# An attention and mixture-of-experts block: queries and keys projected feature-major, tile fronts ranked ahead, modulation rows spread by DMA

## The chip, the cores and the metric

The kernel runs as one program on one core of a Trainium2 chip. The metric is device time in microseconds (us) of one execution. The engines are named as in the profile: PE is TensorE's matrix multiply and PEld its weight loads, DVE is VectorE, ACT is ScalarE, POOL is GpSimd, SP is SyncE, which mostly issues DMA transfers. An engine name with a q (ACTq, SPq) is that engine's instruction queue.

## The reference

A block over 2 sequences of 2048 tokens with 256 features: adaptive layer norm, causal attention with two query heads of 128 that share one key and one value head, and then a dense-weighted mixture of 8 experts. Cut to what matters:

```python
mod = (silu(c) @ wmod).reshape(2, 6, 1, 256)
sa, ca, ga, sb, cb, gb = six rows of mod          # per sequence
ga = (2 * (ga >= 0) - 1) * maximum(abs(ga), 0.25) # gb likewise
h = layernorm(x) * (1 + ca) + sa
q, k, v = rope(h @ Wq.T), rope(h @ Wk.T), h @ Wv.T  # rope turns neighbouring pairs of features
w = softmax(causal(q @ k.T * 128 ** -0.5))
x = x + ga * ((w @ v) @ Wo.T)
h = layernorm(x) * (1 + cb) + sb
gate = softmax(h @ Wg + bg) - sigmoid(h @ Wt + bt) * 0.125   # kept where >= 0, renormalised
x = x + gb * sum over experts of gate_e * (gelu(h @ W1_e + b1_e) @ W2_e + b2_e)
```

All inputs and outputs are 32-bit floats, and so are the matmuls of the projections, scores and experts.

## The kernel before, in words

The program has two stages. `attention` works through 32 tiles of 128 tokens (16 in each sequence); `experts` then runs over lists of the tokens that each expert was given.

**How the order comes about.** In `attention` nothing is issued when the Python code passes it. Each step is handed to a `Plan` with `plan.add(engine, cost, what to do, after=..., take=..., give=..., rank=...)`. `Plan.run` plays a list schedule with these costs: whenever an engine is free, it takes the ready step of lowest rank, provided that the buffers it takes are free by the counts in `room`. What comes out is a fixed order of instructions on each engine; on the chip each engine follows its order strictly and waits on semaphores. `late` is an allowance for a transfer's landing. `first` is the rank -100 for the steps of the start.

**A tile** (`tile_steps`) has rank `r`, and all its steps share that rank. It loads x on SP, takes mean and variance (`moments`: L432 and L434 on DVE, L438 and L439 on POOL), normalises (`xn`, L468 on DVE or POOL), turns the tile by two PE transposes (`turn`, L477), and applies scale and shift while it copies to hT (L485 on ACT, L487 on DVE). `qkv` (L498) multiplies hT, as the stationary side, with the joined weight matrix of 512 columns: two matmuls with 512 moving columns. An f32 matmul is executed as two passes, so that is four records in the trace. The result lies with tokens on the partitions. `rot` forms the rotation from it on DVE (L514, L520, L523), the two products are added on DVE or POOL (L529), and `turn_rot` (L536) turns the two queries and the key by three PE transposes so that features lie on the partitions; `qT_out` (L539, L541) copies them out on ACT, the queries scaled by 128 ** -0.5.

The rest of a tile is scores (`score`, L552, and the mask by a bf16 matmul, L556), maximum (L563 and L570 on DVE), exponential (L579 on ACT), transposes of the probabilities (L625) and copies (L629), the product with the values (`pav`, L635), a copy (L663), the output projection (`po`, L669), the residual sum (L676), the second norm (`hx`, L692 and L695), a store of the token's features in planes of 16 bits (`halves`, L702) and the gating logits (`pl`, L739). After every group of up to four tiles `gate_steps` works out which experts take each token, and POOL scatters entries into the list of expert 0 (L852).

**Modulation.** `by_feature` (L342) gives the first norm's scale and shift with features on the partitions. For each of the two sequences, `gates` (L365) and `rows` (L393) multiply c, copied over 128 columns (`sc_bc`, L333), with the other modulation weights, so that every partition receives the same rows; `gates_out` (L374 to L388) applies sign and minimum on all 128 partitions and folds the gate into the output weights woG.

**Buffers.** Six PSUM banks serve as "ps", two as "pav"; 16 score buffers "s", 9 input tiles "x".

**The end of attention.** Steps of rank 1000 work on two items of expert 0 ahead (`pha` L1007, `pya` L1024) while the last tiles' gating, lists and gathers run. Then `experts` starts.

Of the kernel before, what the change touches and what calls it, by code (L numbers as in the profile page):

```python
# [12 lines left out]
F32 = mybir.dt.float32  # L13
# [8 lines left out]
P = 128  # L22
# [17 lines left out]
MASKED = -3.0e38  # L40
HB = 6
# [162 lines left out]
def attention(  # L204
# [9 lines left out]
            "hT": 2, "hT2": 2, "hpT": 2, "aT": 2, "g_sb": 1, "sign": 1, "size": 1, "ga": 1}  # L214
    const = ctx.enter_context(tc.tile_pool(name="const_a", bufs=1))
    pool = ctx.enter_context(tc.tile_pool(name="work", bufs=3))
    small = ctx.enter_context(tc.tile_pool(name="small", bufs=8))
# [9 lines left out]
    def little(shape, tag, u, dtype=F32):  # L227
        return small.tile(shape, dtype, tag=tag, name=f"{tag}{u}")
# [19 lines left out]
    wqkv_sb = const.tile([P, KD, 4 * HS], F32, name="wqkv_sb")  # L248
# [5 lines left out]
    rope_sb = const.tile([P, NT, 2, HS // 2], F32, name="rope_sb")  # L254
# [5 lines left out]
    wo_sb = wpool.tile([P, NH, D], F32, tag="w2_0", name="wo_sb")  # L260
    sc_bc = wpool.tile([P, KD, B, P], F32, tag="w1_0", name="sc_bc")
# [12 lines left out]
    nc.vector.tensor_copy(back[:, 0, :], ids)  # L274
    nc.gpsimd.memset(kept.front, 0.0)
    nc.gpsimd.memset(entry, 0.0)
    nc.gpsimd.tensor_copy(
        entry[:, :, :, 2].bitcast(I32), ids.unsqueeze(2).to_broadcast([P, NTOK // P, E])
    )
    for z in (1, 0):  # L280
        nc.vector.tensor_scalar(back[:, z, :], back[:, 0, :], float(z - NTOK), None, ALU.add)
# [8 lines left out]
    def idle_work(many):  # L290
        pi = ps_tile(f"pi{many}")
        for _ in range(many):
            nc.tensor.matmul(pi[:, :P], ident, ident, start=True, stop=True)

    plan.add("PE", 5.0, lambda: idle_work(12), take=["ps"], give=["ps"], rank=first - 5)
# [4 lines left out]
    l_m0 = load(wm_0, wm[:, :, : 2 * D], 512, rank=first - 1)  # L300
    l_qkv = load(wqkv_sb, wqkvT.rearrange("(k p) f -> p k f", p=P), 512, rank=first - 1)
    l_rope = [
        load(rope_sb[:, ds(4 * q, 4)], rope.rearrange("(q n p) (z f) -> p q n z f", p=P, n=4, z=2)[:, q],
             256, rank=first if q == 0 else q * 8 - 7.5)
        for q in range(NT // 4)
    ]
# [13 lines left out]
    def load_expert(e):  # L320
# [10 lines left out]
    s_bc = plan.add(  # L331
        "DVE", 0.6,
        lambda: nc.vector.tensor_copy(sc_bc, sc.unsqueeze(3).to_broadcast([P, KD, B, P])),  # L333
        after=[s_sc], rank=first,
    )
# [22 lines left out]
    m_wo, m_mod, m_gb = [], [], []  # L358
    for b in range(B):

        def gates(b=b):
            box["pg", b] = pg = ps_tile(f"pg{b}")
            for g, which in enumerate((2, 5)):
                for k in range(KD):
                    nc.tensor.matmul(  # L365
                        pg[:, ts(g, D)], sc_bc[:, k, b, :], wm_1[:, k, ts(which - 2, D)],
                        start=(k == 0), stop=(k == KD - 1),
                    )

        def gates_out(b=b):  # L370

            u = f"_g{b}"
            g_sb = work([P, 2 * D], "g_sb", u)
            nc.vector.tensor_copy(g_sb, box["pg", b])  # L374
            sign = work([P, 2 * D], "sign", u)
            nc.vector.tensor_scalar(sign, g_sb, 0.0, 2.0, ALU.is_ge, ALU.mult)
            size = work([P, 2 * D], "size", u)
            nc.vector.scalar_tensor_tensor(size, g_sb, -1.0, g_sb, ALU.mult, ALU.max)
            nc.vector.tensor_scalar(size, size, 0.25, None, ALU.max)
            ga = work([P, D], "ga", u)  # L380
            nc.vector.scalar_tensor_tensor(
                ga, sign[:, :D], 1.0, size[:, :D], ALU.subtract, ALU.mult
            )
            nc.vector.scalar_tensor_tensor(
                gb_bc[:, b, :], sign[:, D:], 1.0, size[:, D:], ALU.subtract, ALU.mult
            )
            for h in range(NH):
                nc.vector.tensor_tensor(woG[:, b, h, :], wo_sb[:, h, :], ga, ALU.mult)  # L388

        def rows(b=b):  # L390
            box["pr", b] = pr = ps_tile(f"pm2{b}")
            for k in range(KD):
                nc.tensor.matmul(  # L393
                    pr, sc_bc[:, k, b, :], wm_1[:, k, D : 3 * D],
                    start=(k == 0), stop=(k == KD - 1),
                )

        def rows_out(b=b):
            pr = box["pr", b]
            nc.vector.tensor_copy(mod_bc[:, b, :D], pr[:, :D])  # L400
            nc.vector.tensor_scalar(mod_bc[:, b, D:], pr[:, D:], 1.0, None, ALU.add)

        r = 1.6 + 3 * b
        g = plan.add("PE", 1.8, gates, after=[s_bc, l_m1], take=["ps"], rank=r)
        m_wo.append(plan.add("DVE", 4.0, gates_out, after=[g, l_wo], give=["ps"], rank=r))
        g = plan.add("PE", 1.8, rows, after=[s_bc, l_m1], take=["ps"], rank=r)
        m_mod.append(plan.add("DVE", 0.9, rows_out, after=[g], give=["ps"], rank=r))

    prev, l_first = [], []
    for e in range(RES):  # L410
        prev = [
            plan.add(
                "SP", 6.0, lambda e=e: load_expert(e), after=m_wo + m_mod + [m_T] + prev, late=2.0,
                rank=8.0 + 4 * e,
            )
        ]
        l_first += prev
# [26 lines left out]
    def tile_steps(b, i, r, group, g):  # L444
# [9 lines left out]

        def load_x():
            st["x"] = work([P, D], "x", u)
            nc.sync.dma_start(st["x"], x[b, ts(i, P), :])
# [6 lines left out]
        n_n = moments("a" + u, st, [n_x], add)  # L464
# [7 lines left out]
        n_n = add(["DVE", "POOL"], [0.42, 1.3], xn, [n_n], take=["xn"])  # L472
# [16 lines left out]
        n_t = add("PE", 0.32, turn, [n_n], take=["ps"], give=["xn"])  # L489
        n_0 = add("ACT", 0.27, lambda: hT(0, "ACT"), [n_t, m_T], take=["hT"])  # L490
        n_1 = add(
# [3 lines left out]
        def qkv():  # L495
            st["pq"] = ps_tile(f"pq{u}")
            for k in range(KD):
                nc.tensor.matmul(  # L498
                    st["pq"], st["hT"][:, k, :], wqkv_sb[:, k, :],
                    start=(k == 0), stop=(k == KD - 1),  # L500
                )

        n_q = add("PE", 1.75, qkv, [n_0, n_1, l_qkv], take=["ps"], give=["hT"])
        n_v = add("ACT", 0.27, lambda: nc.scalar.copy(v[:, i, :], st["pq"][:, 3 * HS :]), [n_q])
        ready_v[b, i] = n_v


        def rot(z):
            dst = st["t", z] = work([P, 3, HS], f"t{z}", u)
            table = rope_sb[:, i, z, :]  # L510
            src = st["pq"][:, : 3 * HS].rearrange("p (h j two) -> p h j two", h=3, two=2)
            d4 = dst.rearrange("p h (j two) -> p h j two", two=2)
            if z == 0:
                nc.vector.tensor_tensor(  # L514
                    d4, src,
                    table.unsqueeze(1).unsqueeze(3).to_broadcast([P, 3, HS // 2, 2]), ALU.mult,
                )
            else:
                t3 = table.unsqueeze(1).to_broadcast([P, 3, HS // 2])
                nc.vector.scalar_tensor_tensor(  # L520
                    d4[:, :, :, 0], src[:, :, :, 1], -1.0, t3, ALU.mult, ALU.mult
                )
                nc.vector.tensor_tensor(d4[:, :, :, 1], src[:, :, :, 0], t3, ALU.mult)  # L523

        n_r0 = add("DVE", 0.6, lambda: rot(0), [n_q, l_rope[i // 4]], take=["big"])
        n_r1 = add("DVE", 0.75, lambda: rot(1), [n_q, n_v, n_r0], give=["ps"])
        n_r = add(
            ["DVE", "POOL"], [0.58, 1.0],
            lambda eng: of[eng].tensor_tensor(st["t", 0], st["t", 0], st["t", 1], ALU.add),  # L529
            [n_r0, n_r1],  # L530
        )

        def turn_rot():
            st["pr"] = ps_tile(f"pr{u}")
            for h in (2, 0, 1):
                nc.tensor.transpose(st["pr"][:, ts(h, P)], st["t", 0][:, h, :], ident)  # L536

        def qT_out():
            nc.scalar.copy(kT[:, ts(i, P)], st["pr"][:, 2 * P : 3 * P])  # L539
            st["qT"] = work([P, NH, P], "qT", u)  # L540
            nc.scalar.mul(st["qT"].rearrange("p h t -> p (h t)"), st["pr"][:, : NH * P], scale)  # L541

        n_t = add("PE", 0.48, turn_rot, [n_r], take=["ps"], give=["big"])
        n_k = add("ACT", 0.65, qT_out, [n_t], take=["qT"], give=["ps"])
# [13 lines left out]
        def keep(h, c):  # L558
            w = min(SC, n - c * SC)
            s = st["s", h, c] = work([P, SC], "s", f"{u}_{h}_{c}")  # L560
            if ("mx", h) not in st:
                st["mx", h] = little([P, 4], "mx", f"{u}_{h}")
            nc.vector.tensor_scalar(  # L563
                s[:, :w], st["sc", h, c][:, :w], 1.0, None, ALU.mult, ALU.max,
# [22 lines left out]
        for h in range(NH):  # L587
            kept = []
            for c in range(nch):
                w = min(SC, n - c * SC)  # L590
                n_s = add(
                    "PE", w * 0.0017 + (0.12 if c == nch - 1 else 0.0),
# [107 lines left out]
        def halves():  # L700
# [4 lines left out]


        by_dma = r < NTOK // P - 4
        n_f = add("POOL", 0.8, halves, [n_h], take=["hp"], give=["hx"] if by_dma else [])
        n_hp = add(
            "SP", 0.5,  # L710
            lambda: nc.sync.dma_start(
# [815 lines left out]
```

## Time and profile before

| | |
|---|---|
| median of 3 runs | 1637.64 us (1635.61 to 1640.75) |
| the profiled execution: time and span | 1637.52 us and 1635.4 us |
| granted PE clock, mean | 0.996 |
| PE busy | 1610.8 us, 98% of the span |
| PE weight loads busy | 1343.9 us, 82% |
| DVE, ACT, POOL busy | 663.0, 572.4, 913.9 us |
| matmuls of the chain that ended last: experts (L1224 and L1234) | 35% and 35% of the span |
| the same: pav L635, psc L552, ptr L625, pq L498, po L669, pr L536 | 6%, 6%, 3%, 3%, 1%, 0% |

The span is from the first instruction to the last; the time of the execution is some 2 us more. The expert stage starts near 480 us. PE's records overlap: a matmul's printed duration holds the time until its result is out, while the next one has already begun. The distance from start to start tells what it occupies.

### The profile page before, as it was taken

What the parts mean: (1) busy time and instruction counts of PE and PEld (TensorE: products, weight loads), DVE (VectorE), ACT (ScalarE), POOL (GpSimd) and SP (SyncE); (2) the same over time, 40 slices, a digit from 0 to 9 for tenths busy, and PEclk for the clock granted to TensorE, in tenths of its full rate; (3) what the DMA queues carried; (4) which work ended last, traced back from release to release, by engine and by line L of the source; (5) the groups of instructions that cost most, each with busy time, mean ns of one, the idle gap of its engine ahead of it and who ended that gap; (6) DMA issues with size and microseconds to landing.
All of it is one profiled execution on the core that took longest, in us unless ns stands there. A gap on an engine that the chain in (4) does not pass through costs nothing.

```text
span 1635.4 us, 26058 instructions
## 1 busy us (share of the span) xinstructions
PE 1610.8 (98%) x7652; PEld 1343.9 (82%) x7652; DVE 663.0 (41%) x2165; ACT 572.4 (35%) x1385; POOL 913.9 (56%) x1045
## 2 busy tenths in 40 slices
PE   9999999999999999999999999999999999999997
PEld 6667776777778888888888888888888888888886
DVE  7887757665532232223223232222332232222322
ACT  3555555556532222222223222222222222222321
POOL 4675433231127767747767775775777477644443
PEclk9999999999999999999999999999999999999999
DMA  5521111020033353335335333533534333333333
GB/s 162 167 57 43 40 36 36 23 47 17 14 85 58 60 118 60 60 67 111 56 69 110 58 63 58 110 56 59 110 58 66 58 59 59 65 62 55 64 56 49
DMA packets 181180, 108.97 MB, mean 67 GB/s; under 512 B 126272, under 2 KB 172480, under 8 KB 180992
## 3 DMA queue, kind: packets, MB, share of 16 engines
q0 software_dynamic: 41968, 46.83, 18.0%
q1 hardware_dynamic: 131280, 48.85, 13.2%
q10 hardware_dynamic: 7872, 12.58, 2.3%
q8 instruction: 26, 0.43, 0.1%
q14 instruction: 34, 0.28, 0.1%
HBM read 49.34 MB, written 31.86 MB: 50 GB/s over the span
## 4 chain that ended last, share of the span: by engine, by line
PE 91%; DVE 3%; POOL 2%; issue 1%; DMA 1%; ACT 1%; another core or an unknown queue 0%; POOLq 0%; SPq 0%; DVEq 0%; ACTq 0%
PE h L1224 35%; PE y L1234 35%; PE pav L635 6%; PE psc L552 6%; PE ptr L625 3%; PE pq L498 3%; PE po L669 1%; PE pya L1024 1%; PE pha L1007 1%; DMA list<-entry,place 1%; PE pl L739 1%; POOL list L852 1%; DVE s L563 0%; DVE x L676 0%; PE pr L536 0%
## 5 line engine op out<-in xcount | busy, mean ns | idle before, releaser
L1259 ACT ACTIVATE g<-h,b_sb 128x256 f32<-128x256 f32 (+1 forms) x688 | 317.8, 465 | 836.4 <-PE h L1224 733.4
L1234 PE MATMUL y<-w,g 128*128 128x256 f32 x2640 | 584.8, 379 | 1.5 <-ACT g L1259 1.5
L1224 PE MATMUL h<-xT,w 128*128 128x256 f32 (+1 forms) x2752 | 584.9, 371 | 0.0
L1224 PEld LDWEIGHTS h<-xT,w 128*128 128x128 f32 x2752 | 506.0, 190 | 66.5 <-DVE xT L1287 0.9
L1234 PEld LDWEIGHTS y<-w,g 128*128 128x128 f32 x2640 | 500.5, 190 | 70.8 <-ACT g L1259 3.1
L1383 POOL DMA_INDIRECT out<-yo,who x172 | 282.9, 1645 | 211.7 <-DVE yo L1326 157.3
L1373 POOL DMA_INDIRECT list<-new,to x216 | 220.7, 1022 | 93.6 <-issue 53.8
L1311 DVE TENSOR_TENSOR yb<-y,b_bc 128x256 f32<-128x256 f32 x165 | 62.7, 419 | 425.1 <-PE y L1234 354.6
L1349 POOL DMA_INDIRECT xr<-feats,at x172 | 173.7, 1010 | 100.5 <-POOL at L1394 70.5
L1287 DVE COPY xT<-xp 128x512 uint16<-128x512 uint16 x172 | 69.3, 445 | 321.0 <-DMA xp<-xr 170.7
L635 PE MATMUL pav<-pT,v 128*128 128x256 f32 x544 | 143.4, 386 | 0.5 <-ACT pT L629 0.5
L552 PE MATMUL psc<-kT,qT 128*128 128x512 f32 (+3 forms) x320 | 142.6, 531 | 0.3 <-ACT pT L629 0.3
L635 PEld LDWEIGHTS pav<-pT,v 128*128 128x128 f32 x544 | 95.7, 190 | 30.7 <-issue 18.4
L563 DVE TENSOR_SCALAR_CACHE_REDUCE s<-psc 128x512 f32<-128x512 f32 (+3 forms) x160 | 95.6, 605 | 60.3 <-PE psc L552 38.6
L579 ACT ACTIVATE s<-s,nmx 128x512 f32<-128x512 f32 (+3 forms) x160 | 103.7, 650 | 43.1 <-DVE nmx L570 42.9
L629 ACT COPY pT<-ptr 128x512 f32<-128x512 f32 (+1 forms) x144 | 76.1, 565 | 47.4 <-PE pav L635 32.1
L852 POOL DMA_INDIRECT list<-entry,place x40 | 42.4, 1059 | 81.2 <-DVE place L849 62.8
L625 PEld LDWEIGHTS ptr<-ident,s 128*128 128x128 f32 x544 | 62.9, 141 | 18.4 <-ACT s L579 7.1
L1302 DVE SCALAR_TENSOR_TENSOR gate<-gb_bc,mcur,part 128x256 f32<-128x256 f32 x172 | 75.7, 481 | 3.0
L625 PE MATMUL ptr<-ident,s 128*128 128x128 f32 x544 | 71.9, 274 | 3.3 <-ACT s L579 3.0
L552 PEld LDWEIGHTS psc<-kT,qT 128*128 128x128 f32 x320 | 57.6, 190 | 15.3 <-issue 7.0
L1394 POOL COPY at<-sheet 128x2 int32 x85 | 60.7, 714 | 9.7 <-DMA xp<-xr 9.7
(172 smaller groups left out, 1052.3 us busy)
## 6 DMA issues: line engine op xcount, KB each, us to landing
w<-in_w ACTq DMA_DIRECT2D x12, 1024.0 KB
x<-in_x SPq DMA_DIRECT2D x32, 128.0 KB, 2.0
out<-x SPq DMA_DIRECT2D x32, 128.0 KB, 1.7
feats<-hp SPq DMA_DIRECT2D x32, 128.0 KB, 1.7
w<-in_w SPq DMA_DIRECT2D x4, 1024.0 KB, 6.5
list<-new,to POOLq DMA_INDIRECT x216
xr<-feats,at POOLq DMA_INDIRECT x172
out<-yo,who POOLq DMA_INDIRECT x172
```

Source lines behind the costliest of these rows:

```text
L552: nc.tensor.matmul(ps[:, :w], st["qT"][:, h, :], kT[:, ds(c * SC, w)], start=True, stop=not last)
L563: nc.vector.tensor_scalar(s[:, :w], st["sc", h, c][:, :w], 1.0, None, ALU.mult, ALU.max, accum_out=st["mx", h][:, c : c + 1],)
L579: nc.scalar.activation(s[:, :w], s[:, :w], AF.Exp, bias=st["nmx", h], accum_out=st["den"][:, h, c : c + 1],)
L625: nc.tensor.transpose(ptr[:, j, h, :], s[:, ds((c0 + j) * P % SC, P)], ident)
L629: nc.scalar.copy(pT[:, :m], st["ptr", c0][:, :m])
L635: nc.tensor.matmul(st["pav"][:, : NH * P], v[:, c0 + j, :], st["pT", c0][:, j].rearrange("p h t -> p (h t)"), start=(c0 + j == 0), stop=(c ...
L1224: last = pe.matmul(hs[f % HB][:, :w], weights[e][0][:, k, ts(f, P)], xT[:, k, :w], start=(k == 0), stop=(k == KD - 1),)
L1234: last = pe.matmul(ys[c], gs[f][:, ts(c, P)], weights[e][1][:, f, :], start=(f == 0), stop=(f == NF - 1),)
L1259: act.activation(gs[f][:, :w], hs[f % HB][:, :w], AF.Gelu_apprx_tanh, bias=b1_sb[:, at : at + 1],).then_inc(sem["act"], 1)
L1349: pool.indirect_dma_start(out=xr[:, ts(c, 2 * D)], out_offset=None, in_=feats, in_offset=bass.IndirectOffsetOnAxis(ap=at[:, c : c + 1], ax ...
L1373: pool.indirect_dma_start(out=lists[e], out_offset=bass.IndirectOffsetOnAxis(ap=to[:, j : j + 1], axis=0), in_=new[:, j, :], in_offset=Non ...
L1383: pool.indirect_dma_start(out=rows, out_offset=bass.IndirectOffsetOnAxis(ap=who[:, c : c + 1], axis=0), in_=yo[:, c, :], in_offset=None, b ...
```

## The change

1. *Queries and keys by features.* The weights of queries and key become the stationary side and hT the moving side: for each of the three heads and the two halves of the features a matmul with 128 moving columns, whose result has features on the partitions. The values are still made with tokens on the partitions, in two matmuls of 128 columns. The turn-back transposes and their copies are gone. The weights' columns are reordered on chip (`order_columns`) so that the even features come first and the odd ones second; rotation is then two products with a table of features by tokens and a swap of the two halves of 64 partitions, which ACT copies. The scale moves into the maximum step. The rotation table doubles in size.
2. *Fronts ranked ahead.* The steps of a tile from the first norm to the maxima get rank `r - LEAD`, LEAD being 5.
3. *Modulation's rows on two partitions.* c itself (two columns) is the stationary side, for both sequences at once. Sign and minimum are worked out on two partitions; the rows are stored to memory, and three transfers on SP's queue spread them over the 128 partitions.
4. *First weights on ACT's queue.* The transfer of wm_0 is issued by ACT.
5. Besides: the first fills of `entry` and `back` become steps of the plan, the warm-up has 8 matmuls instead of 12, several costs that the plan uses are changed, and two small tiles get fewer buffers.

```diff
+LEAD = 5
...
+    wv_sb = const.tile([P, KD, HS], F32, name="wv_sb")
...
+    wqk_sb = const.tile([P, KD, 3, HS], F32, name="wqk_sb")
+    rope_sb = const.tile([P, 2, T], F32, name="rope_sb")
...
+    own = [plan.add("POOL", 1.7, entries, rank=1.0), plan.add("DVE", 0.9, places_back, rank=1.0)]
...
-    plan.add("PE", 5.0, lambda: idle_work(12), take=["ps"], give=["ps"], rank=first - 5)
+    plan.add("PE", 3.4, lambda: idle_work(8), take=["ps"], give=["ps"], rank=first - 5)
...
-    l_m0 = load(wm_0, wm[:, :, : 2 * D], 512, rank=first - 1)
-    l_qkv = load(wqkv_sb, wqkvT.rearrange("(k p) f -> p k f", p=P), 512, rank=first - 1)
...
+    l_m0 = plan.add(
+        "ACT", 0.5, lambda: nc.scalar.dma_start(wm_0, wm[:, :, : 2 * D]), late=4.5, rank=first - 6
+    )
+    wqkv = wqkvT.rearrange("(k p) f -> p k f", p=P)
+    l_qk = load(wqk_in, wqkv[:, :, : 3 * HS], 384, rank=first - 1)
+    l_v = load(wv_sb, wqkv[:, :, 3 * HS :], 128, rank=first - 1)
...
-    s_bc = plan.add(
-        "DVE", 0.6,
-        lambda: nc.vector.tensor_copy(sc_bc, sc.unsqueeze(3).to_broadcast([P, KD, B, P])),
-        after=[s_sc], rank=first,
-    )
+    def order_columns(k, eng):
+        src = wqk_in[:, k].rearrange("p (h j two) -> p h j two", h=3, two=2)
+        dst = wqk_sb[:, k].rearrange("p h (two j) -> p h j two", two=2)
+        if eng == "ACT":
+            nc.scalar.copy(dst, src)
+        else:
+            nc.vector.tensor_copy(dst, src)
...
+    def rows(h):
+
+        pr = box["pr", h] = ps_tile(f"pm2{h}")
+        for k in range(KD):
+            nc.tensor.matmul(
+                pr[:B, :], sc[:, k, :], wm_1[:, k, ts(h, 2 * D)],
+                start=(k == 0), stop=(k == KD - 1),
+            )
...
+    def spread(dst, g, many):
+        nc.sync.dma_start(dst, rows_dram[:, g * D : (g + many) * D].partition_broadcast(P))
...
+    n = plan.add("DVE", 2.2, rows_ready, after=m_out, rank=r)
+    n = plan.add(
+        "SP", 0.5, lambda: nc.sync.dma_start(rows_dram, by_row.rearrange("b g d -> b (g d)")),
+        after=[n], rank=r, late=2.0,
+    )
+    m_ga = plan.add("SP", 0.7, lambda: spread(ga_bc, 2, 1), after=[n], rank=r, late=2.0)
...
+        def lead(eng, cost, do, after=(), **how):
+
+            return plan.add(eng, cost, do, after=after, rank=r - LEAD, **how)
...
         def qkv():
-            st["pq"] = ps_tile(f"pq{u}")
+            pq = st["pq"] = ps_tile(f"pq{u}")
+
+            for h in range(3):
+                for k in range(KD):
+                    nc.tensor.matmul(
+                        pq[:, ts(h, P)], wqk_sb[:, k, h, :], st["hT"][:, k, :],
+                        start=(k == 0), stop=(k == KD - 1),
+                    )
             for k in range(KD):
                 nc.tensor.matmul(
-                    st["pq"], st["hT"][:, k, :], wqkv_sb[:, k, :],
+                    pq[:, 3 * P :], st["hT"][:, k, :], wv_sb[:, k, :],
                     start=(k == 0), stop=(k == KD - 1),
                 )
...
-        def turn_rot():
-            st["pr"] = ps_tile(f"pr{u}")
-            for h in (2, 0, 1):
-                nc.tensor.transpose(st["pr"][:, ts(h, P)], st["t", 0][:, h, :], ident)
...
+        def swap():
+            sw = st["t", 1] = work([P, 3, P], "t1", u)
+            half = HS // 2
+            src = st["pq"][:, : 3 * P].rearrange("p (h t) -> p h t", h=3)
+            nc.scalar.copy(sw[:half], src[half:])
+            nc.scalar.copy(sw[half:], src[:half])
+
+        def rot_sum(eng):
             st["qT"] = work([P, NH, P], "qT", u)
...
+            t0, t1 = st["t", 0], st["t", 1]
+            of[eng].tensor_tensor(kT[:, ts(i, P)], t0[:, 2, :], t1[:, 2, :], ALU.add)
+            of[eng].tensor_tensor(st["qT"], t0[:, :NH, :], t1[:, :NH, :], ALU.add)
...
-        n_t = add("PE", 0.48, turn_rot, [n_r], take=["ps"], give=["big"])
-        n_k = add("ACT", 0.65, qT_out, [n_t], take=["qT"], give=["ps"])
+        n_r0 = lead("DVE", 0.6, lambda: rot(0), [n_q, l_rope[i]], take=["big"])
+        n_r1 = lead("ACT", 0.95, swap, [n_q, n_v, n_r0], give=["ps"])
+        n_r1 = lead("DVE", 0.55, lambda: rot(1), [n_r1])
+        n_k = lead(
+            ["DVE", "POOL"], [0.7, 1.2], rot_sum, [n_r0, n_r1], take=["qT"], give=["big"]
+        )
```

## The prediction

> **What bounds the kernel now.** I read the busy time by stretch first, to see which engine sets each stage; the columns are length, then PE, weight loads, DVE, ACT and POOL busy (with counts), granted clock, DMA share and GB/s.
>
> ```profile
> 0.00:20.00 20.00, 18.12 (x81) 13.42 (x82) 12.46 (x34) 4.53 (x12) 8.45 (x28) 0.91 0.90 283
> 20.00:120.00 100.00, 96.35 (x445) 64.32 (x445) 85.93 (x323) 53.07 (x161) 64.46 (x97) 1.00 0.34 100
> 120.00:400.00 280.00, 279.03 (x1355) 199.42 (x1354) 186.22 (x698) 159.65 (x439) 102.99 (x149) 1.00 0.14 36
> 400.00:480.00 80.00, 74.71 (x379) 60.31 (x378) 37.59 (x169) 37.42 (x88) 11.00 (x15) 1.00 0.07 20
> 480.00:1635.00 1155.00, 1142.63 (x5399) 1006.40 (x5397) 340.78 (x945) 317.76 (x688) 727.05 (x757) 1.00 0.39 71
> ```
>
> Attention runs to 480 us and the experts from there to the end. The change touches attention alone, and PE is busy there for all but 1.9 + 3.7 + 1.0 + 5.3 us. Busy alone could hide slack, so I read next, in order of time, what PE does and how far apart its groups start.
>
> ```profile
> 9.40 5.35 PE L498 MATMUL pq<-wqkv_sb,hT 128*128 128x512 f32 x8 [0.38 <-ACT hT L485]
> ...
> 33.13 1.94 PE L498 MATMUL pq<-wqkv_sb,hT 128*128 128x512 f32 x4
> 34.90 1.02 PE L552 MATMUL psc<-kT,qT 128*128 128x512 f32 x2
> 35.76 0.22 PE L556 MATMUL psc<-maskb,identb 128*128 128x128 bf16 x1
> 35.82 1.94 PE L393 MATMUL pm<-wm,sc_bc 128*128 128x512 f32 x4
> 37.59 1.02 PE L552 MATMUL psc<-kT,qT 128*128 128x512 f32 x2
> ...
> 57.46 0.82 PE L536 MATMUL pr<-ident,t 128*128 128x128 f32 x6
> 58.11 1.10 PE L669 MATMUL po<-woG,aT 128*128 128x256 f32 x4
> ```
>
> Groups start one right behind another: the next begins while the one before still drains, so the cost of a group is the distance to the next start, not its printed duration. By that measure a tile's projection costs 34.90 - 33.13 = 1.77 us (others: 1.71, 1.72), one of the four modulation groups 37.59 - 35.82 = 1.77, and a turn-back transpose (58.11 - 57.46) / 6 = 0.11. The price of many short matmuls, each with its own weight load, comes from these:
>
> ```profile
> 6.61 1.92 PE L342 MATMUL pm<-sc,wm 128*128 128x2 f32 x16
> ...
> L342 PE MATMUL pm<-sc,wm 128*128 128x2 f32 x16 | 1.9, 250 | 0.1
> L536 PE MATMUL pr<-ident,t 128*128 128x128 f32 x96 | 15.4, 274 | 0.0
> ```
>
> Sixteen f32 passes, each with a 128x128 load, take 1.92 us with the last one's 0.25 of latency: (1.92 - 0.25) / 15 = 0.111 us from start to start, though only two columns move. That is the rate of the loads. Last, what PE waits for:
>
> ```profile
> PE ptr L625 <- ACT s L579: 3.0, 2, 1.9
> PE pl L739 <- POOL hT L727: 0.7, 1, 0.7
> PE pav L635 <- ACT pT L629: 0.5, 1, 0.5
> ```
>
> No single wait carries attention; PE's own passes do. So a pass removed there should come off the end.
>
> **The change, step by step.** The profiled execution took 1637.52 us (span 1635.4 and 2.1 around it), 0.1 under the median of 1637.64; the sum is made against 1637.5.
>
> *Turn-back transposes removed* (L536): 32 tiles x 3 x 0.11 = 10.5 us off PE. The copies that followed them on ACT (0.263 and 0.393) go too.
>
> *Projection in short passes.* A tile had 2 matmuls of 512 columns, 4 passes; now it has 8 of 128 columns, 16 passes with a load each. At 0.111 this is 1.78 against 1.71 to 1.77 (mean 1.74): +0.04 x 32 = +1.3 us. The bounds: columns alone (the same 2048 pass-columns) +0; at the mean duration of one f32 load, 190 ns, if a load hid behind nothing, 3.04 a tile and +42 us. I take 0.111, since the 16 rows are the very load and only their moving side is narrower; a 128-column pass moves in 1.72 / 16 = 0.108, less than that.
> The Trainium skill (TensorE: Matmul & The Clock Gate, Back-to-back issue gap) speaks against this edit: in a stream of load and matmul pairs it gives about 81 ns a matmul at 128 columns where the moving side alone would need 56. With two passes to an f32 matmul that would be an estimate of 2.6 us a tile, +28 us over 32 tiles, and the kernel would be slower; the transposes and the sixteen passes above don't show such a surcharge.
>
> *Modulation on two partitions.* Four groups of 1.72 to 1.77 become two of the same 512 columns: -3.5 us on PE. On DVE, two rounds of 0.69 + 0.43 + 0.69 + 0.43 + 0.42 + 0.42 + 0.76 + 0.42 + 0.41 and the 0.39 broadcast give way to one of about 2.7, two of 0.76 and one reorder of weights (0.56): about 5 us less, in the stretch where DVE is 86% busy. ACT gets four small copies and the other reorder, 2 us; its cover is 47 idle us in 20 to 120.
> New is a chain: rows, copies, DVE, store to memory, then three spreads (256, 512, 256 KB) on SP's queue. The first projection needs the first spread. In the new order six tiles' projections (10.7 us), eight input turns (1.8), two rows groups (3.5), eight scores with masks (4.7) and 2.0 of others stand ahead of it on PE: 23 us from the first projection, about 33 us of span. The chain: rows end near 20, DVE 2.7 and its queue to 24, store and spread at the 2.0 median of a 128 KB load plus issue, 29, gates 0.76 behind other DVE work, 31. So it is hidden, by some 2 us. If each transfer took the 5.3 us that loads show in the first 60 us, the two are 6.6 later, and PE loses about 5. DVE would stand at the gates, with the maxima and rotations of later tiles behind it, and SP would hold the first stores and expert 0's weights, none due for 15 us. I take 0, bound +5.
>
> *Rotation.* DVE's 0.350 + 0.347 become one 128x384 product (0.565, as the sum's row); the swapped halves come from two ACT copies of 64x384, between the 0.39 of 256 elements and 0.565 of 512, about 0.48 each. ACT gains 0.96 and loses 0.66 a tile, +10 us in all, against 120 idle us in 120 to 400. The sum, now in two pieces, goes to POOL for 20 tiles and to DVE for 12 (it was 22 and 10); POOL's 1.0 becomes about 1.2. PE waits for none while other tiles' products are in its queue. Cost 0; if that cover is gone, up to 1 us a tile in the eight early tiles, +8.
>
> *Fronts ranked ahead.* Statistics, projection and scores of a tile are ordered as if five tiles earlier. What it can win is PE's idle time: 3.7 us in 20 to 120, 1.0 in 120 to 400, 1.9 of the wait for ACT late on. What it can lose is as large: the 16 score buffers and 9 inputs may be held by fronts while a tile's later steps want DVE. I take -2, with -6 and +8.
>
> *Start.* The first modulation weights leave from ACT's queue near 0.7 instead of SP's at 2.23, so their matmuls may begin near 5 instead of 6.6. But on DVE the scale and shift copy now stands behind the statistics of the third and fourth input, and the weights' reorder behind its load. Those inputs land after 1664 KB instead of 1792; at some 380 GB/s, with the first 512 KB begun earlier, near 8.2 instead of 9.1. Two rounds of 0.43 + 0.18, the copies 0.23 and the first scaled half 0.46 put the first projection at about 9.8: +0.4. Its first eight passes now take 5.35 us where eight later take 3.54, at a granted clock of 0.91 over the first 20 us; whether that repeats is open, so -1.8 to +1.8. The warm-up shrinks from 24 passes to 16 of about 0.21, which end at 4.8, still before the weights land: 0.
>
> *Transfers and the rest.* The rotation table doubles to 2 MB and the spreads read 1 MB: about 5 us of queue at 380 GB/s, ahead of nothing due before 30. The postponed fills of POOL and DVE (1.6 and 1.9 us) are due only at the first gating. The tail after the last input turn keeps its order.
>
> Sum: -10.5 + 1.3 - 3.5 - 2 + 0.4 = -14.3, so **1623.2 us**; I give 1623.
>
> **Rivals.**
> *A, more comes:* the new order also closes the gaps and the start meets no low clock: -6 instead of -2, -1.8 at the start: 1617. For it: only 1.0 us idle in 280 where buffers are plentiful. Against: DVE at 86% early.
> *B, the saving returns as waits:* in the first 120 us DVE or the spreads, not PE, set the pace; +8 from the order and +5 from the chain leave about 1636, no change. For it: DVE's 86% and the 90% DMA share. Against: DVE's own load falls by 5 us.
> *C, slower:* the load of a pass doesn't hide behind a 128-column pass. Place: 16 passes of every tile. It decides from 14.3 / 512 = 0.028 above the 0.111, so from 0.139 a pass; at 0.190 it is 40 above the forecast, 1664. Against it: 0.111 in sixteen rows.
> *D, the ranks do nothing,* since inputs or score buffers run out: without the 2, 1625, inside the forecast. The written order speaks against it: six projections now precede the first output projection, before there were four.
>
> **How the numbers follow.** Forecast with D 0.68, its own range 1616 to 1633; A 0.10; B 0.13; C 0.09. No change is within 0.3%, 4.9 us, about what a measurement of this kernel can tell. Faster: 0.67 + 0.10 + 0.03 of B = 0.80. Same: 0.01 + 0.07 = 0.08. Slower: 0.03 + 0.09 = 0.12. The range reaches from A to B with the runs' own spread of some 3 us at either end, 1614 to 1640; it leaves out C and the worst of B.
>
> **What would show it.** In the profile after: no transposes of rotated tiles; a projection of 16 passes whose next group starts 1.8 us on (2.6 or more: C); two rows groups; attention's end near 466 instead of 480 and the same 1155 us behind it; PE's idle time in 20 to 120 at or under 4 us (over 10: B); the first projection near 10 us. I am wrong if PE waits on the gates, on the swapped copies or on a spread.

## The result and the profile after

The changed kernel took 1622.47 us, median of four runs (1620.81 to 1624.62), against 1637.15 for the kernel before on the same chip: a ratio of 0.9908, with a 95% interval of 0.9886 to 0.993. The forecast was 1623. Its profiled execution took 1623.79 us, with a span of 1621.6.

The view of the whole by stretch, of the changed kernel, with the edges at its own stages. Columns: length, then PE, weight loads, DVE, ACT and POOL busy (with counts), granted clock, DMA share, GB/s.

```profile
0.00:20.00 20.00, 17.43 (x95) 16.55 (x96) 9.70 (x27) 5.87 (x13) 8.45 (x28) 1.00 0.90 291
20.00:120.00 100.00, 97.72 (x579) 75.92 (x578) 85.23 (x310) 67.94 (x186) 61.41 (x100) 1.00 0.39 116
120.00:390.00 270.00, 269.15 (x1474) 206.37 (x1473) 190.84 (x694) 163.44 (x421) 105.61 (x159) 1.00 0.14 38
390.00:466.50 76.50, 72.80 (x387) 60.41 (x386) 39.55 (x174) 33.69 (x78) 16.29 (x21) 1.00 0.10 26
466.50:1621.00 1154.50, 1142.09 (x5388) 1004.69 (x5386) 339.34 (x941) 318.00 (x688) 726.55 (x757) 1.00 0.39 71
```

The difference lies in attention: the first matmul of the experts starts at 465.4 us, where it started at 480.6, and from there to the end of the span it is 1156.2 us, where it was 1154.8. PE is idle for 2.3 us between 20 and 120 (before 3.7) and for 0.85 between 120 and 390, although ACT has become busier early (67.94 against 53.07 us) and the weight loads too (75.92 against 64.32).

The order of time on PE shows what a tile's projection and a group of modulation rows cost now:

```profile
19.87 3.60 PE L399 MATMUL pm<-wm,sc 128*2 128x512 f32 x8
...
28.18 1.56 PE L548 MATMUL pq<-hT,wqk_sb 128*128 128x128 f32 x12
29.57 0.61 PE L553 MATMUL pq<-wv_sb,hT 128*128 128x128 f32 x4
30.02 0.60 PE L683 MATMUL pav<-pT,v 128*128 128x256 f32 x2
```

From the projection's first pass to the next group's start it is 30.02 - 28.18 = 1.84 us (another tile: 1.78); it was 1.71 to 1.77. Sixteen passes at 0.111 to 0.115 thus pass as sixteen passes of 128 columns would by themselves: the weight load of each hides behind the pass ahead of it. The modulation rows are two groups in 3.6 us, where four took 4 x 1.77 = 7.1. There are no transposes of rotated tiles.

The start, from the same view with all engines. A bracket gives the idle time before the group and what ended it:

```profile
0.73 0.48 ACTq L321 DMA_DIRECT2D wm<-in_wmod  x1
4.48 0.20 ACT L357 ACTIVATE sc<-c_sb 128x4 f32<-128x4 f32 x1 [1.94 <-DMA c_sb<-in_cT]
5.58 3.54 PE L379 MATMUL pm<-sc,wm 128*128 128x2 f32 x16 [0.44 <-DMA wm<-in_wmod]
7.29 0.83 DVE L365 COPY wqk_sb<-shared 128x384 f32<-128x384 f32 x1 [0.26 <-DMA shared<-in_wqkvT]
9.83 0.20 DVE L387 TENSOR_SCALAR modT<-pm 128x4 f32<-128x4 f32 x2
11.34 2.77 PE L548 MATMUL pq<-hT,wqk_sb 128*128 128x128 f32 x12
```

The modulation matmuls do begin an us earlier, at 5.58, but they take 3.54 us where they took 1.92, and the twelve passes of the first projection take 2.77 instead of 1.56: PE runs at half pace until about 16. The first projection starts at 11.34, before the change at 9.40. The column of the granted clock says 1.00 for this stretch because the clock's records of this execution begin at 16.2 us; here the spacing of the passes is the better witness.

Last, what PE waits for in attention behind the start (total, times, longest):

```profile
PE pt L525 <- DVE xn L516: 2.2, 1, 2.2
PE psc L600 <- DVE thr L853: 0.8, 1, 0.8
PE pya L1072 <- DVE yo L1079: 0.5, 1, 0.5
PE pav L683 <- ACT pT L677: 0.3, 1, 0.3
```

It waits neither for the gates, nor for the swapped copies, nor for a spread. One wait of 2.2 us for an input turn, near 33 us, is all that is large.

### The profile page after: what moved, and what is told of

The parts are those of the page before. It is cut to its first block, busy times and chain, and to the rows that moved or that the text cites. A ratio compares the mean times of both kernels' runs of the same rounds, so it can differ in the third digit from the quotient of the medians.

```text
span 1621.6 us, 26590 instructions
## 1 busy us (share of the span) xinstructions
PE 1599.2 (99%) x7916; PEld 1363.9 (84%) x7916; DVE 664.7 (41%) x2141; ACT 589.0 (36%) x1385; POOL 918.3 (57%) x1063
## 4 chain that ended last, share of the span: by engine, by line
PE 95%; POOL 1%; DVE 1%; issue 1%; DMA 1%; ACT 1%; POOLq 0%; another core or an unknown queue 0%; SPq 0%; ACTq 0%; DVEq 0%
PE h L1272 35%; PE y L1282 34%; PE pav L683 7%; PE psc L600 7%; PE ptr L673 3%; PE pq L548 2%; PE po L717 2%; PE pya L1072 1%; PE pha L1055 1%; PE pq L553 1%; PE pl L787 1%; POOL list L900 0%; PE pt L525 0%; DMA x<-in_x 0%; DMA out<-yo,who 0%
## 5 line engine op out<-in xcount | busy, mean ns | idle before, releaser
L673 PE MATMUL ptr<-ident,s 128*128 128x128 f32 x544 | 77.1, 273 | 0.0
L1374 DVE TENSOR_TENSOR yo<-yb,gate 128x512 f32<-128x512 f32 (+1 forms) x85 | 57.0, 671 | 3.7
```

What stands on the lines that cost most here:

```text
L673: nc.tensor.transpose(ptr[:, j, h, :], s[:, ds((c0 + j) * P % SC, P)], ident)
```

## The experiments

The ratios below are to the kernel before, measured on the same chip in turn with it; 0.001 is 1.6 us. Two kernels compared with each other are compared by these ratios. The changed kernel's own interval, 0.9886 to 0.993, is 3.6 us to either side, so a difference to the changed kernel is good to some 4 us either way, and one between two of the others to some 2.

**One part undone at a time.** First the transposes alone: three of them per tile put back, with nothing reading them.

```
+        def unread():
+            pz = ps_tile(f"pz{u}")
+            for h in range(3):
+                nc.tensor.transpose(pz[:, ts(h, P)], ident, ident)
+        lead("PE", 0.33, unread, [n_q], take=["ps"], give=["ps"])
```

> The changed kernel, with three PE transposes of the identity added behind every tile's projection, into a bank that nobody reads: the transposes that the change took out, without their readers. Theory (PE's own passes set attention's length): 96 x 0.11 = 10.5 us come back, about 1633 us, and attention ends near 476 us of span instead of 466. Rival (the gain came from something else, and PE has room): under 3 us come back, 1622 to 1625.

Ratio 0.997 [0.9962, 0.9979], 0.0062 or 10.2 us above the changed kernel. In the order of time on PE such a group moves the next start by 135.75 - 135.42 = 0.33 us:

```profile
135.42 0.49 PE L565 MATMUL pz<-ident 128*128 128x128 f32 x3
135.75 1.02 PE L606 MATMUL psc<-kT,qT 128*128 128x512 f32 x2
```

So 32 x 0.33 = 10.6 us of PE's passes cost 10.2 us of time, give or take 4: one for one as far as the runs can tell, as forecast (10.5).

Then the whole old projection with its weights in their own order, its rotation table, rotation and transposes, in the new order of fronts and with the new modulation:

```
-                        pq[:, ts(h, P)], wqk_sb[:, k, h, :], st["hT"][:, k, :],
...
+                    st["pq"], st["hT"][:, k, :], wqkv_sb[:, k, :],
...
+                nc.tensor.transpose(st["pr"][:, ts(h, P)], st["t", 0][:, h, :], ident)
```

> The changed kernel with the projection of before: tokens on the partitions, four passes of 512 columns, rotation on DVE, three transposes back and copies on ACT; ranks, modulation and start stay as changed. Theory: 10.5 us of transposes come back, 32 x 0.05 to 0.09 = 1.6 to 2.9 us of short passes go, and the start loses its reorder copies (about -1): about 1629. Rival (short passes cost what the transposes cost): 1622 or less.

Ratio 0.9975 [0.9966, 0.9984]: with the new order the new projection is worth 0.0067, 11.0 us. The transposes and the passes had been put at -10.5 + 1.3 = -9.2, within the runs' 4 us of it.

The old modulation, on 128 partitions, in the new kernel:

```
-                pr[:B, :], sc[:, k, :], wm_1[:, k, ts(h, 2 * D)],
...
+                    pr, sc_bc[:, k, b, :], wm_1[:, k, D : 3 * D],
```

> The changed kernel with the modulation of before: four groups on PE, signs and minima on 128 partitions, no store and spreads. Theory: 3.5 us of PE passes come back, about 1626. Rival (the spreads' chain cost PE as much as the two groups saved): 1622 to 1623, or less.

Ratio 0.9946 [0.9933, 0.996], 0.0038 or 6.2 us above the changed kernel. In the order of time on PE the products that keep it busy ahead of the experts (`pi`) are the mark for attention's end. First the kernel with the old modulation:

```profile
465.64 1.35 PE L310 MATMUL pi<-ident 128*128 128x128 f32 x10 [1.42 <-issue]
468.37 2.04 PE L1290 MATMUL y<-ident 128*128 128x128 f32 x8 [1.37 <-issue]
```

and the changed one:

```profile
461.68 1.35 PE L312 MATMUL pi<-ident 128*128 128x128 f32 x10 [1.41 <-issue]
464.40 1.13 PE L1294 MATMUL y<-ident 128*128 128x128 f32 x8 [1.37 <-issue]
```

Attention ends 4.0 us later in these two executions, for a forecast of 3.5; 0.9 more is in the second line, the same eight products at half pace (2.04 for 1.13 us). What is then left of the 6.2 is within the 4 us of the comparison. Such stretches of half clock are taken up at the end.

**The ranks.** `LEAD = 5` set to `LEAD = 0`, all else as changed:

> The changed kernel with LEAD = 0: fronts have their tile's own rank again. Theory of the prediction: the ranks are worth 2 us, so about 1624.5, and PE's idle time in 20 to 120 us rises from 2.3 to about 4. Rival 1: the ranks do nothing, 1622.5. Rival 2: they carry what the slower start gives away, 5 us or more, 1627 to 1630.

Ratio 1.0011 [1.0002, 1.002]: not faster than the kernel before at all. The lead is worth 0.0103, 16.9 us, where the prediction had 2. Is that the lead itself, or the lead together with the new projection? Two kernels ask it from the other side: the kernel before with nothing but the lead,

```
+LEAD = 5
+            return plan.add(eng, cost, do, after=after, rank=r - LEAD, **how)
```

> The kernel before with one edit: the steps of a tile from the first norm to the maxima are ranked five tiles ahead, at the plan's old costs. Theory 1 (ranks can win back only the waits that a kernel has, and before PE waited little between 20 and 470 us): 2 to 6 us faster than before, 1631 to 1635. Theory 2 (ranks are worth the 17 us that the run without them lost, whatever else is changed): about 1621. Theory 3 (they help only the new projection): 1636 to 1638.

which gave 0.9979 [0.9969, 0.9988], 3.4 us; and the changed kernel with the old projection and no lead:

> The changed kernel with the projection of before and LEAD = 0: what is left of the change is the modulation, the start and the plan's new costs. Theory 1 (the new projection's front is what needs the ranks): 3.5 us of modulation are kept, 1633 to 1637, faster than the new projection without ranks (1639.5). Theory 2 (ranks are worth 17 us to either projection): 1648 to 1652. Theory 3 (the new costs or the start are at fault for the waits without ranks): 1640 or more, with PE's waits spread as in the run without ranks.

0.997 [0.9958, 0.9982]. With the four ratios side by side (new modulation in all):

| | lead 0 | lead 5 |
|---|---|---|
| old projection | 0.9970 | 0.9975 |
| new projection | 1.0011 | 0.9908 |

With the old projection and the new modulation the lead does nothing that can be measured. With the new projection it decides: without it the new projection is 0.0041 (6.7 us) slower than the old, though PE has fewer passes to do; with it, 0.0067 faster. The two parts can't be priced apart. Nor can the lead and the modulation: the lead alone gave the kernel before 3.4 us and the modulation with the new start and costs 4.9 (0.9970), yet both together, with the old projection, give 4.1 (0.9975).

Where the time goes without the lead is read by stretch, here of the kernel with lead 0 and new projection:

```profile
20.00:120.00 100.00, 93.81 (x572) 75.06 (x572) 87.06 (x313) 59.88 (x163) 59.92 (x96) 1.00 0.43 123
120.00:300.00 180.00, 178.19 (x1007) 139.33 (x1006) 125.54 (x442) 109.84 (x286) 76.64 (x121) 1.00 0.15 37
300.00:460.00 160.00, 154.45 (x780) 117.22 (x779) 91.26 (x379) 92.42 (x232) 36.55 (x53) 0.99 0.10 26
```

and of the changed kernel, in the two last of these stretches (the first of them is above):

```profile
120.00:300.00 180.00, 179.16 (x1007) 139.11 (x1005) 132.15 (x474) 109.62 (x284) 84.41 (x130) 1.00 0.15 40
300.00:460.00 160.00, 159.08 (x831) 124.47 (x829) 95.22 (x386) 87.52 (x215) 35.89 (x49) 1.00 0.11 30
```

PE stands idle for 6.2 us instead of 2.3 in the first, and for 5.5 instead of 0.9 in the last. Between 20 and 460 it is busy for 9.5 us less (426.45 for 435.95), and the `pi` products start at 477.7 instead of 461.7; the rest of the 16.9 us is not accounted for in full, but a window of half clock at 434.6 us is a part of it. It is no one wait; the list of waits of the kernel without lead is long and even:

```profile
PE pl L787 <- POOL hT L775: 1.9, 3, 1.2
PE ptr L673 <- DVE col L890: 1.5, 1, 1.5
PE ph L767 <- DVE hx L743: 1.4, 1, 1.4
PE ptr L673 <- ACT s L627: 1.4, 2, 0.9
PE psc L600 <- POOL qT L585: 1.1, 1, 1.1
PE pq L548 <- ACT hT L533: 1.0, 3, 0.5
```

My explanation at this point was the length of the new front: from the end of a tile's last projection pass to its finished queries it takes 12.2 us in the median without the lead and 5.3 with it. If that chain (ScalarE, VectorE, GpSimd in turn) is what is late for the scores, shortening it must help without any lead, and a smaller lead should do as well as 5. Both were tried. This kernel has lead 0 and leaves the swap of halves out, so the rotation is not the reference's:

```
-            nc.scalar.copy(sw[:half], src[half:])
-            nc.scalar.copy(sw[half:], src[:half])
...
-                src = st["t", 1]
+                src = st["pq"][:, : 3 * P].rearrange("p (h t) -> p h t", h=3)
```

> The changed kernel without lead and without the swap of halves: the second product reads the projection itself, so the rotation is left out in part (two ScalarE copies a tile, 0.95 us, and one change of engine less). Theory: without lead the new projection costs 17 us because the chain from projection to queries (ScalarE, VectorE, GpSimd in turn) is late for the scores: shortened by the swap it gives back a third to a half, ratio 0.993 to 0.997, and the median from the projection's end to the queries falls from 12 to under 9 us. Rival: it is the order in TensorE's queue, not the chain's length: ratio 1.000 to 1.002.

Ratio 0.9979 [0.997, 0.9989]. The chain's median fell from 12.2 to 6.0 us, nearly as short as in the changed kernel, and 0.0032 (5.2 us) came back of the 16.9. Then `LEAD = 2`:

> The changed kernel with the fronts ranked 2 ahead in place of 5 (0 gave a ratio of 1.0011, 5 gives 0.9908). Theory: what counts is that the chain from a projection to its queries is out of the way before the tile's scores are due, which takes some 5 us when nothing is queued ahead of it and 10 to 16 in the order without a lead; a lead of 2 ranks is one tile's time of 15 to 25 us in the later tiles and covers that: ratio 0.991 to 0.993. Rival: the gain is proportional to the lead: 0.997.

Ratio 0.9949 [0.9936, 0.9962]: of the 16.9 us, 10.2 come with the first two ranks and 6.7 with the next three, so neither answer is right. Its chain has a median of 5.9 us, and still it is 0.0041 (6.7 us) slower than with 5. So the chain's length explains a part at most: two kernels with nearly as short a chain as the changed one are 7 and 12 us slower. What they share with lead 0 is idle time of PE, and in different places. First the kernel with lead 2, then the one without the swap:

```profile
120.00:300.00 180.00, 176.54 (x971) 135.59 (x970) 123.52 (x433) 107.19 (x277) 83.14 (x130) 1.00 0.15 39
300.00:460.00 160.00, 159.07 (x839) 123.31 (x838) 98.88 (x402) 94.05 (x236) 36.48 (x51) 1.00 0.10 26
```

```profile
20.00:120.00 100.00, 97.83 (x603) 78.52 (x602) 87.14 (x316) 51.81 (x150) 68.28 (x107) 1.00 0.43 125
120.00:300.00 180.00, 177.36 (x983) 138.27 (x983) 122.02 (x437) 98.43 (x260) 79.69 (x121) 1.00 0.15 38
300.00:460.00 160.00, 153.47 (x797) 117.47 (x796) 91.12 (x388) 86.58 (x219) 35.24 (x50) 1.00 0.09 24
```

The shorter chain did win back the early stretch: without the swap PE is idle there for 2.2 us, as in the changed kernel, where it was 6.2. The two kernels without lead, one with the swap and one without it, lose most late, 5.5 and 6.5 us of 160, and their last projection pass starts at 319.9 and 333.9 us: no projection is left to fill PE while the last tiles are finished. With lead 5 it starts at 351.8, with lead 2 at 370.1, and there the late stretch loses 0.9 us. The old projection without lead agrees: its last pass starts at 356.3, and it loses 2.0:

```profile
300.00:460.00 160.00, 157.97 (x787) 119.03 (x786) 95.34 (x400) 91.13 (x234) 32.72 (x46) 1.00 0.10 26
```

That fits the idle time, and it was not tried by a kernel of its own. What stays open is why the planner's order without the lead fits the old projection (PE 435.32 us busy of 440 between 20 and 460) and not the new one (426.45), with a median chain of 12 us in both, and why it does the last of the new projections so much earlier.

**The spread of the modulation rows.** The prediction took this chain as hidden by some 2 us. Two more trips of its 8 KB through memory lengthen it:

```
+        "SP", 0.5, lambda: nc.sync.dma_start(hops[0], by_row.rearrange("b g d -> b (g d)")),
+        "SP", 0.01, lambda: nc.sync.dma_start(hops[1], hops[0]), after=[n], rank=r,
+        "SP", 0.01, lambda: nc.sync.dma_start(rows_dram, hops[1]), after=[n], rank=r,
```

> The changed kernel, with the 8 KB of modulation rows copied through DRAM twice more before they are spread (computes the same). Two more transfers of 8 KB put some 4 us (two of about 2 us) into the chain from the rows to the scaled output weights. The prediction holds that this chain is hidden by about 2 us: then 0 to 2 us more than the changed kernel, ratio to the kernel before 0.991 to 0.992, and the first output projection waits up to 2 us. Rival 1, it is not hidden: 4 us more, ratio 0.9933. Rival 2, the order of TensorE's other work moves far enough to cover all of it: ratio 0.9908 and no wait at the first output projection.

Ratio 0.99 [0.9884, 0.9916], the same as the changed kernel's. The chain in order of time, of the changed kernel:

```profile
28.61 0.31 SPq L440 DMA_DIRECT2D rows<-shared  x1
30.00 0.39 SPq L430 DMA_DIRECT2D shared_o<-rows  x1
35.67 0.91 DVE L427 TENSOR_TENSOR woG<-shared_o 128x256 f32<-128x256 f32 x2
38.82 1.08 PE L717 MATMUL po<-woG,aT 128*128 128x256 f32 x4
```

and with the two trips:

```profile
27.30 0.32 SPq L441 DMA_DIRECT2D hop<-shared  x1
28.70 0.60 SPq L445 DMA_DIRECT2D hop<-hop  x1
30.78 0.47 SPq L448 DMA_DIRECT2D rows<-hop  x1
32.85 0.40 SPq L431 DMA_DIRECT2D shared_o<-rows  x1
36.45 0.76 DVE L428 TENSOR_TENSOR woG<-shared_o 128x256 f32<-128x256 f32 x2 [2.01 <-DMA shared_o<-rows]
37.51 1.08 PE L724 MATMUL po<-woG,aT 128*128 128x256 f32 x4
```

From the first store to the spread's issue it is 5.55 us instead of 1.39: 4.2 us more. VectorE then waits 2.01 us for the spread, and the first output projection does not: it starts 10.21 us behind the first store in both kernels (37.51 - 27.30 and 38.82 - 28.61). The cover is at least 4 us, twice what was forecast; with the two trips it is nearly used up, for the scaled weights are ready at 37.21.

**The start.** Twelve warm-up products instead of eight, so that PE is still busy when the first weights land:

```
-    plan.add("PE", 3.4, lambda: idle_work(8), ...
+    plan.add("PE", 5.0, lambda: idle_work(12), ...
```

> The changed kernel with 12 warm-up matmuls instead of 8. In the changed kernel the sixteen passes of the first modulation ran 0.22 us apart where they ran 0.11 apart before. Theory (the pause of 0.75 us behind the short warm-up keeps PE slow, but the first projection waits for DVE's statistics, not for these passes): the sixteen passes take 1.9 us again, the first projection still begins near 11 us, at most 0.5 us is gained. Rival (the slow passes delay the start): 2 us gained, 1620.5.

Ratio 0.9897 [0.9883, 0.9912]. And the first modulation weights back on SP's queue, behind the small input and two tiles:

```
-        "ACT", 0.5, lambda: nc.scalar.dma_start(wm_0, wm[:, :, : 2 * D]), late=4.5, rank=first - 6
+    l_m0 = load(wm_0, wm[:, :, : 2 * D], 512, rank=first - 1)
```

> The changed kernel with the first modulation weights issued by SP, behind the first two inputs, as before. Theory (on ACT's queue they only took the place of c and the inputs, which landed 0.8 to 1.8 us later): the inputs' statistics begin near 5.0 instead of 5.9 and the first projection within 0.7 us of 11.3; 1622 to 1623.5, no difference. Rival (the prediction's view, earlier weights help): 1624 or more.

Ratio 0.9899 [0.9885, 0.9913]. Each is 1 to 2 us under the changed kernel and within its interval. That ACT's queue carries the first weights wins nothing that can be measured: the first projection starts at 11.10 with SP and at 11.34 with ACT.

Last a kernel meant to beat both, with the twelve products, five more behind the modulation's columns, and the third and fourth tile's statistics behind the modulation's copy on VectorE:

```
+    plan.add("PE", 1.2, lambda: idle_work(5), after=[m_pe], take=["ps"], give=["ps"], rank=first - 4)
-        n_n = moments("a" + u, st, [n_x], lead)
+        n_n = moments("a" + u, st, [n_x] + [m_T] * (r in (2.0, 3.0)), lead)
```

> The changed kernel with 12 warm-up products in place of 8, 5 more between the modulation's columns and the first projection, and the statistics of the third and fourth tile behind the modulation's columns on VectorE (computes the same). Theory: the first projection starts at about 10.2 us in place of 11.3 and its passes stand 0.111 apart in place of 0.213: 2.5 to 3.5 us less than the changed kernel, ratio to the kernel before 0.9885 to 0.9893. Rival: the start is bound by the inputs and the early front of the first tiles, so that it gives no more than the 12 warm-up products alone: 0.9895 to 0.9900.

The start became what the theory said; its order of time on PE has

```profile
6.63 2.16 PE L379 MATMUL pm<-sc,wm 128*128 128x2 f32 x16
8.90 1.28 PE L312 MATMUL pi<-ident 128*128 128x128 f32 x10
10.24 1.50 PE L549 MATMUL pq<-hT,wqk_sb 128*128 128x128 f32 x12
```

with the first projection at 10.24 and twelve passes in 1.50 us instead of 2.77. The time did not follow: ratio 0.9893 [0.9878, 0.9907], and on the same chip the kernel with the two extra trips, whose start was left alone, took 1623.76 us against 1623.97. The order of time shows where part of the gain may have gone; it is of the slowest of this kernel's four executions (1626.37 us), so the others need not show it:

```profile
65.24 1.13 PE L684 MATMUL pav<-pT,v 128*128 128x256 f32 x4 [0.73 <-ACT pT L678]
68.23 0.58 PE L788 MATMUL pl<-wgt_sb,hT 128*128 128x9 f32 x4 [1.86 <-DVE hT L776]
68.67 2.87 PE L549 MATMUL pq<-hT,wqk_sb 128*128 128x128 f32 x12
71.34 1.00 PE L554 MATMUL pq<-wv_sb,hT 128*128 128x128 f32 x4
```

The changed order brings a new wait of 1.86 us for the routing, and behind it the clock is granted at 0.5 from 68.7 to 72.1: the same twelve passes take 2.87 us. It beats the kernel before, as the changed kernel does, and the changed kernel by nothing that these runs can tell.

## Why the prediction was right, and where it was not

The total was right (1622.5 for 1623), and the reading that carried it too: attention is bound by PE's passes, so a pass taken off comes off the end. But the sum is right in part by luck. It prices the projection as if its cover were there, and the lead at 2 us, without having seen that the first depends on the second. Take the lead first, and the terms stand: with the old projection it gives nothing, and the new projection then gives 11.0. Take the projection first, as the middle rows do, and two terms are wrong by some 15 us in opposite directions.

| step | forecast, us | measured, us |
|---|---|---|
| turn-back transposes | -10.5 | -10.2 |
| projection, passes, rotation and transposes together, with the lead | -9.2 | -11.0 |
| the same without the lead | -9.2 | +6.7 |
| modulation on two partitions | -3.5 | -4.0 by attention's end, -6.2 by the ratios |
| the lead, with the new projection | -2 | -16.9 |
| first projection's start | +0.4 | +1.9 |
| all, by the ratio | -14.3 | -15.1 |

The measured rows overlap and don't add up to the last; those taken from the ratios are good to some 4 us, "the same without the lead" to some 2.

- *Transposes and short passes*: right, and for the reason given. The sixteen rows of two columns, 0.111 apart, were the right price for a pass with its own load: 0.111 to 0.115 came out. Rival C (slower from 0.139 a pass) is excluded. The prediction's estimate of 2.6 us a tile takes twice 81 ns for each of the sixteen passes; sixteen times 81 would be 1.3 us. On the rule that was weighed there (the Trainium skill, TensorE: Matmul & The Clock Gate, Back-to-back issue gap), these f32 passes show no surcharge of the kind.
- *Rotation, "cost 0; if that cover is gone, up to +8"*: this step failed as it was put. With the new projection the cover is there only with the lead. Without it the new projection, forecast to gain 9.2, loses 6.7: 15.9 us more than the forecast, twice the bound. How much of that is the rotation isn't shown; leaving its swap out gave 5.2 back.
- *Fronts ranked ahead, "-2, with -6 and +8"*: failed where the new projection is in, and outside its bounds. It was priced from the idle time in the profile of before, 3.7 + 1.0 + 1.9 us, as if the other edits left that idle time as it was. But what the lead wins is idle time that the new front would make and that the profile of before can't show. On the kernel before, it is worth 3.4 us, near the forecast. Rival D (the ranks do nothing, 1625) is wrong by far: the kernel without them took 1639.5 us.
- *Modulation*: the size right by attention's end; the ratios give 2.7 more, within their 4 us. The gates' chain was hidden, as claimed, by at least 4 us, not 2.
- *Start*: the sign right, the size short by 1.5 us. Three things were missed: the small input `c` comes later when the big transfer leaves first from ACT's queue (it ends ACT's wait at 4.48, and at 2.67 with that transfer on SP's); the reorder copies take 0.83 and 0.87, where 0.56 was assumed; and behind the shortened warm-up, priced at 0, PE runs at half pace until 16 us.
- *Rival A* (1617) is not what happened, *rival B* (waits take it back, 1636) is what would have happened without the lead, and more: the saving went back as small waits of PE on every other engine, and not on the spreads. Nor were they waits of the early stretch alone, as B has it: 5.5 us lie behind 300 us, and the longest in the list are for steps behind the scores.

## What to carry to other kernels

When a change both takes work off the binding engine and lengthens the chain that feeds it, price the new order and the new work together: here, with the new modulation in place, the order alone gave nothing, the new projection alone cost 6.7 us, and both together gave 10.2 (0.9970 to 0.9908). A reorder's worth can't be read from the idle time of the old kernel, since the idle time that it prevents is that of the new one. Of a bound engine's own passes the old trace tells the price to a tenth of an us, from the row nearest in form, even where that row moves far fewer columns.

## What the runs showed of the hardware

- A wait of PE may cost more than its length. In the profiles of six of these kernels the clock was granted at 0.5 for 3.4 us in the middle of attention or just ahead of the experts, each time behind waits of PE of 1.3 to 1.9 us; in the kernel meant to beat both it happened twice, at 68.7 and 464.7 us, and doubles the distance of the passes (2.87 us for twelve instead of 1.50), some 1.7 us each time. It isn't certain: the changed kernel waits 2.2 us near 33 us and 1.4 twice before the experts, and the kernel before 1.9 us at 433.6, with no such window. The Trainium skill (TensorE: Matmul & The Clock Gate, Part 1: The HAM clock gate) gives a free-running window of 3413 ns, and the records agree with that length; it has the clock fall after an idle window of about 3.4 us, and here it fell behind waits of less than 2 us each.
- At the start, sixteen f32 passes of two columns did not bring the clock up: in the changed kernel the passes behind them still stand 0.213 apart until 16 us, and with more products of 128 columns ahead of and behind them 0.111 from 10.24 on. Those products also fill pauses of PE, so the two columns and the pauses aren't told apart.
- Where the records of the clock begin late (16.2 us in the changed kernel), the column of the granted clock shows 1.00 for a stretch in which the passes stand at half pace.
